# A two-layer graph network on one core: filler by three running sums, another order of groups, and paired products in float32r

## The chip, the core and the metric

The kernel runs on one core of a Trainium2 chip. A core has a matrix engine (PE, whose weight loads are listed apart as PEld), a vector engine (DVE), a scalar engine (ACT), a general engine (POOL), which here starts the indirect gathers, and a sync engine (SP), which starts most other transfers. PE writes to PSUM; the other memory on the chip is SBUF. The metric is the device time of one execution in microseconds (us).

## The reference

12,500 nodes with 256 features, 200,000 edges sorted by their target `dst`. Two layers of the same kind, a last product, the residual and a layer norm:

```python
def _sage_conv(x, src, dst, W_l, b_l, W_r):
    agg = segment_sum(x[src], dst, num_segments=12500)
    deg = segment_sum(ones, dst, num_segments=12500)
    mean = agg / maximum(deg, 1.0)[:, None]
    return mean @ W_l + b_l + x @ W_r

h = relu(_sage_conv(x, src, dst, W1_l, b1, W1_r))
h = relu(_sage_conv(h, src, dst, W2_l, b2, W2_r))
x = layernorm(x + h @ W3 + b3)
```

`dst` is drawn as 12500 u² with u uniform, so low nodes have many edges (the first 256 nodes more than a tenth of all) and high nodes few; `src` is uniform.

## The kernel before

Nodes are handled in 98 blocks of 128. Two ways of summing run side by side.

**Gathers**, for nodes with few edges (from node 1280 in layer 1, from 2048 in layer 2). A round (`Gathers.gathered`) fetches four tiles of 128 source rows with four indirect DMAs from POOL into one of four buffers `got` (L262); then PE multiplies each by a 128 x 32 matrix of ones and zeros into a strip of `part_ps` (L274). ACT copies a finished group to `some` (L284), PE spreads it to nodes (L290), DVE adds it to the ring `sums` (L304). Layer 1 has 269 such rounds (1076 gathers), layer 2 has 235 (940). A buffer is written again once PE's strips of four rounds earlier are done.

**Counts**, for nodes with many edges: groups of 256 target nodes, numbered from 0. `count(g)` builds the matrix C[source node, target node] of how many edges join the two, in bfloat16 as `counts` (98 blocks x 256 columns): per tile of 128 edges DVE makes `pick`, `low` and `aft` by comparison (L738 to L746), PE multiplies them (L765, L776, L780) into `count_ps`, and ACT copies the result into a window of `counts` (L782); for the first 128 tiles DVE adds it instead (L769). The eight groups have 236, 120, 92, 80, 80, 72, 68 and 68 tiles. `product` then sums over the 98 source blocks, rows transposed times C, into `dense_ps` (L707). Rows are float32 values split exactly into three bfloat16 parts by `exact` (two DVE and two ACT steps a block), stored to `x3_d` or `h3_d` in HBM and loaded again two blocks at a time; so each block and group costs six matmuls of 256 columns.

In layer 1, group 0 is counted while all rows of x are split; then group g is counted while the product of group g-1 runs, up to group 5; groups 0 to 4 are multiplied, and the counts of 0 to 3 are stored in HBM (`stored`, L831). Layer 2 makes four passes over the rows of h: pass g (4 to 7) multiplies group g, counted on chip, and beside it group g-4, whose counts are streamed back from HBM (L697), into `beside_ps`; groups 6 and 7 are counted meanwhile.

**Blocks.** When a block's sum is complete, `first_block` or `last_block` runs in pieces: load the rows, transpose on PE (L902), copy on ACT (L904), the products with the weights (L925, L930), bias and degree on DVE (L936, L937), relu on ACT (L939); layer 1 then stores h and its parts, layer 2 goes on with W3 and the layer norm (L993 to L1010).

**The order** on PE and POOL is written out by the program. `layer` goes through the rounds; in each it issues the gathers and strips, and three times takes a piece of a block (`pieces`) and then filler (`fill`): counts, products, splits, taken from generators that yield a cost. The costs are scalars; `mixed` interleaves the parts of a stage in proportion; the whole cost of a layer is spread evenly over its rounds but the last 8 (layer 1) or 14 (layer 2).

Of the kernel before, what the change touches and what calls it, by code (L numbers as in the profile page):

```python
# [1 line left out]

# [5 lines left out]
F32 = mybir.dt.float32  # L8
F16 = mybir.dt.float16
# [38 lines left out]
def by_runs(  # L48
# [66 lines left out]
    def room(t):  # L115
# [16 lines left out]
    h3_d = dram.tile([P, NB, 3, D], BF16, name="h3_d")  # L132
    count_d = dram.tile([HG1 - 1, P, NB, DN], BF16, name="count_d")
# [7 lines left out]
    place = consts.tile([1, len(groups)], I32, name="place")  # L141
# [3 lines left out]
    key_t = [consts.tile([P, n], F32, name=f"key_t{g}") for g, n in enumerate(tiles_of)]  # L145
    after_from = [max(t, FIRST - 1) for t in lows[:HG]]
    after_t = [consts.tile([P, b - a], F32, name=f"after_t{g}")
               for g, (a, b) in enumerate(zip(after_from, highs))]
    offs = [consts.tile([1, n], I32, name=f"offs{g}") for g, n in enumerate(tiles_of)]
# [33 lines left out]
    degs = spare[0:1]  # L183
    rdeg = early.tile([P, NB], F32, name="rdeg")
# [6 lines left out]
    NROWS = 4  # L191
# [114 lines left out]
    with tc.tile_pool(name="setup", bufs=1) as su, \  # L306
# [180 lines left out]
        nxt_first = su.tile([P, HC], F32, name="nxt_first")  # L487
        later(nc.vector.tensor_copy(nxt_first, nxt_i[:, :HC, P - 1]))
        most_c = max(b - a for a, b in spans)
        for g, (c0, c1) in enumerate(spans):  # L490
            n = c1 - c0
            for begins, to, name, since in ((start, key_t[g], "key", lows[g]),
                                            (nxt_first, after_t[g], "aft", after_from[g])):
                at = su.tile([P, HC], F32, name="at", bufs=2)
                nc.vector.tensor_scalar(at[:, :n], begins[:, c0:c1], float(DN * g),
                                        float(DN * (g + 1)), op0=OP.max, op1=OP.min)
                key = su.tile([P, most_c, P], F32, name="key", bufs=2)
                nc.vector.tensor_tensor(key[:, :n], dst_f[:, c0:c1],
                                        at[:, :n].unsqueeze(2).to_broadcast([P, n, P]), op=OP.subtract)
                nc.vector.scalar_tensor_tensor(key[:, :n], key[:, :n], float(NB), high[:, c0:c1],  # L500
                                               op0=OP.mult, op1=OP.add)
                columns(key, (c0, c1), to, name, c0, since, highs[g])

            nc.vector.tensor_scalar(off_f, f1, float(DN * g), float(DN * (g + 1)), op0=OP.max, op1=OP.min)
            nc.vector.tensor_scalar(off_f, off_f, -float(DN * g), None, op0=OP.add)
            nc.vector.tensor_copy(offs[g], off_f[:, lows[g]:highs[g]])
            early_round()
# [64 lines left out]
    w3_sb = weight(w3, "w3_sb", "w3")  # L572

    biases = consts.tile([P, 3, D], F32, name="biases")
    for i, b in enumerate((b1, b2, b3)):
        nc.scalar.dma_start(biases[:, i], b[None, :].to_broadcast([P, D]))
# [9 lines left out]
    split = keep.tile([P, 2, 3, D], BF16, name="split")  # L586
    counts = [keep.tile([P, NB, DN + WIDEST + WIDEST % 2], BF16, name=f"counts{i}") for i in range(2)]
    NEAR = int(at_most(FIRST)) + room(FIRST - 1)
    assert NEAR <= DN
    for c_sb in counts:  # L590
        blank = c_sb.rearrange("p s d -> p (s d)").bitcast(F32)
        nc.scalar.copy(blank, zero.to_broadcast(list(blank.shape)))
# [9 lines left out]
    def layer(gathers, block, n_pieces, dense, dense_cost, left):  # L602
# [3 lines left out]
        turn = 0  # L606

# [7 lines left out]
        def pieces():  # L615
# [5 lines left out]
            if q:  # L621
                next(q[1])
                q[2:] = q[2] - 1, turn + APART
                if q[2] == 0:
                    done.add(q[0])
                    queue.remove(q)
# [3 lines left out]
        spent = 0.0  # L630

        def fill(upto):
            nonlocal spent
            while spent < upto:
                spent += next(filler, 1e9)
# [3 lines left out]
        for i in range(i0, n + 1):  # L639
            before = gathers.step()  # L640

            due = dense_cost * (i + 1 - i0) / (n - i0 - left) if i + 1 < n - left else 1e8
            for part in range(3):
                if part == 2 and before:
                    gathers.summed(*before, done)
                    while begun < left_after(before[0]):
# [3 lines left out]
                fill(spent + (due - spent) / (3 - part))  # L650
        fill(1e8)
# [4 lines left out]
    def exact(t, s, rest):  # L656

# [10 lines left out]
    def split_rows(b):  # L668
        t = load_rows(x, N, b, "split_sb")
        s = split[:, b % 2]  # L670
        leaves = exact(t, s, work.tile([P, D], F32, name="rest", tag="own"))
        if b < 3:
            later(leaves)
        nc.sync.dma_start(x3_d[:, b], s)

    STREAMS = 4
    streams = [spare.bitcast(BF16)[:, i * 2 * DN:(i + 1) * 2 * DN].rearrange("p (b d) -> p b d", b=2)
               for i in range(STREAMS)]
    n_streamed = 0

    def product(table3, g, c_sb, beside=None):


        nonlocal n_streamed
        ps = [dense_pool.tile([P, NC, DN], F32, name="dense_ps")]
        if beside is not None:
            ps.append(beside_pool.tile([P, NC, DN], F32, name="beside_ps"))
        for t in ps:
            nc.tensor.matmul(t, lhsT=zeros_b, rhs=c_sb[:, :NC, :DN], start=True, stop=False)
# [709 lines left out]
```

## Time and profile before

| what | us or share |
|---|---|
| median of 3 runs | 3278.43 (3268.89 to 3285.49) |
| profiled execution | 3281.46, its span 3279.7 |
| granted TensorE clock, mean | 0.888 |
| PE busy | 79% |
| POOL busy | 60% |
| DVE busy | 48% |
| ACT busy | 35% |
| DMA queues q1 (SP) and q0 (POOL) | 34.0% and 26.7% of 16 engines |

Layer 1's rounds begin about 24 us into the span and its last blocks end near 1751; layer 2 begins its gathers at 1753, its products end at 3156. In rows of single instructions the columns are: start and duration in us, engine, line, operation, output <- inputs, and in brackets how long the engine sat idle before it and what ended that. Matmuls overlap, so their durations are longer than their distance from start to start.

### The profile page before, as it was taken

What the parts mean: (1) busy time and instruction counts of PE and PEld (TensorE: products, weight loads), DVE (VectorE), ACT (ScalarE), POOL (GpSimd) and SP (SyncE); (2) the same over time, 40 slices, a digit from 0 to 9 for tenths busy, and PEclk for the clock granted to TensorE, in tenths of its full rate; (3) what the DMA queues carried; (4) which work ended last, traced back from release to release, by engine and by line L of the source; (5) the groups of instructions that cost most, each with busy time, mean ns of one, the idle gap of its engine ahead of it and who ended that gap; (6) DMA issues with size and microseconds to landing.
All of it is one profiled execution on the core that took longest, in us unless ns stands there. A gap on an engine that the chain in (4) does not pass through costs nothing.

```text
span 3279.7 us, 56146 instructions
## 1 busy us (share of the span) xinstructions
PE 2574.5 (79%) x18946; PEld 1733.1 (53%) x18946; DVE 1566.5 (48%) x5560; ACT 1151.6 (35%) x2331; POOL 1967.7 (60%) x2026
## 2 busy tenths in 40 slices
PE   4565668878878878889865887878889888888876
PEld 2122335545546656656643555556556666666654
DVE  6778675544445555555552122334345444343334
ACT  0423664444444444455441001223233333221122
POOL 6665666666665656666664666565666666556652
PEclk9766679979979989989987899989989999999998
DMA  5565668658658758647644566565556656566642
GB/s 123 164 185 171 179 205 274 209 159 262 209 156 289 225 174 266 221 144 238 222 142 122 181 183 184 176 181 166 177 167 192 184 170 183 164 200 198 204 139 84
DMA packets 375242, 612.56 MB, mean 187 GB/s; under 512 B 72111, under 2 KB 253989, under 8 KB 374949
## 3 DMA queue, kind: packets, MB, share of 16 engines
q1 hardware_dynamic: 273235, 343.33, 34.0%
q0 software_dynamic: 96768, 264.37, 26.7%
q8 instruction: 155, 2.54, 0.3%
q10 hardware_dynamic: 4946, 1.19, 0.2%
q14 instruction: 138, 1.13, 0.1%
HBM read 518.75 MB, written 89.92 MB: 186 GB/s over the span
## 4 chain that ended last, share of the span: by engine, by line
PE 59%; issue 8%; another core or an unknown queue 7%; DVE 5%; ACT 3%; DMA 3%; POOL 0%; ACTq 0%; DVEq 0%; SPq 0%; POOLq 0%
PE dense_ps L707 16%; PE part_ps L274 7%; PE count_ps L776 7%; PE beside_ps L707 6%; PE block_ps L925 6%; PE block_ps L930 5%; PE sum_ps L290 4%; PE block_ps L997 3%; PE block_ps L902 3%; DMA rows<-x_d 2%; ACT counts L782 2%; PE count_ps L780 1%; PE sum_ps L296 1%; PE dense_ps L797 1%
## 5 line engine op out<-in xcount | busy, mean ns | idle before, releaser
L262 POOL DMA_INDIRECT got<-in_x_dram,src_t x1076 | 1067.8, 992 | 649.6 <-issue 258.2
L262 POOL DMA_INDIRECT got<-h_d,src_t x940 | 897.7, 955 | 617.1 <-issue 230.8
L707 PE MATMUL dense_ps<-counts,rows 128*128 128x256 bf16 x5292 | 981.6, 282 | 58.9 <-issue 31.5
L707 PEld LDWEIGHTS <-rows 128*128 128x128 bf16 x7644 | 745.2, 101 | 327.6 <-issue 165.6
L782 ACT CAST counts<-count_ps 128x882 f32 (+3 forms) x688 | 611.3, 888 | 533.1 <-PE count_ps L776 135.6
L707 PE MATMUL beside_ps<-spare,rows 128*128 128x256 bf16 x2352 | 570.3, 282 | 24.2 <-issue 23.2
L776 PE MATMUL count_ps<-pick,low 128*128 128x490 bf16 (+2 forms) x1188 | 378.7, 371 | 145.0 <-ACT counts L782 64.3
L274 PE MATMUL part_ps<-got,one 128*32 128x257 f32 (+1 forms) x4032 | 385.4, 434 | 53.2 <-issue 21.7
L738 DVE TENSOR_SCALAR pick<-steps,key_t 128x686 bf16<-128x686 f16 (+3 forms) x816 | 332.6, 410 | 117.6 <-remote 32.1
L218 DVE TENSOR_TENSOR one<-lo_t,lane_b 128x128 f32<-128x128 bf16 x504 | 144.1, 286 | 470.7 <-remote 150.1
L284 ACT COPY some<-part_ps 128x257 f32<-128x257 f32 (+1 forms) x355 | 132.8, 374 | 643.4 <-remote 293.7
L741 DVE TENSOR_SCALAR low<-lanes,low_t 128x130 bf16<-128x130 f16 x816 | 221.0, 272 | 212.4 <-remote 72.5
L304 DVE TENSOR_TENSOR sums<-sums,sum_ps 128x256 f32 x355 | 145.6, 410 | 250.2 <-remote 110.6
L290 PE MATMUL sum_ps<-two,some 128*128 128x128 f32 x1420 | 241.1, 296 | 13.1 <-issue 8.3
L290 PEld LDWEIGHTS sum_ps<-two,some 128*128 128x128 f32 x1420 | 211.2, 207 | 32.2 <-issue 19.3
L776 PEld LDWEIGHTS <-low 128*128 128x128 bf16 x1188 | 121.1, 103 | 181.9 <-issue 62.7
L936 DVE TENSOR_TENSOR own<-block_ps,biases 128x256 f32<-128x256 f32 x196 | 82.4, 420 | 220.3 <-PE block_ps L930 106.5
L274 PEld LDWEIGHTS part_ps<-got,one 128*32 128x32 f32 x4032 | 89.1, 113 | 184.1 <-issue 161.1
L925 PE MATMUL block_ps<-w1l_sb,sums 128*128 128x256 f32 x352 | 123.5, 483 | 69.7 <-issue 31.5
L933 ACT COPY sums<-zero 128x256 f32<-128x256 f32 x170 | 68.7, 404 | 306.0 <-PE block_ps L930 142.6
L904 ACT COPY own_t<-block_ps 128x256 f32<-128x256 f32 x294 | 109.3, 375 | 183.4 <-remote 65.4
L746 DVE TENSOR_SCALAR aft<-steps,after_t 128x98 bf16<-128x98 f16 x689 | 173.6, 252 | 0.0
(184 smaller groups left out, 2678.7 us busy)
## 6 DMA issues: line engine op xcount, KB each, us to landing
rows<-x_d SPq DMA_DIRECT2D x245, 384.0 KB
rows<-h_d SPq DMA_DIRECT2D x196, 384.0 KB
count_d<-counts SPq DMA_DIRECT2D x28, 896.0 KB
spare<-count_d SPq DMA_DIRECT2D x196, 128.0 KB
x_sb<-in_x_dram SPq DMA_DIRECT2D x194, 128.0 KB
x_d<-split SPq DMA_DIRECT2D x98, 192.0 KB
h_d<-split SPq DMA_DIRECT2D x98, 192.0 KB
got<-in_x_dram,src_t POOLq DMA_INDIRECT x1076
```

Of the source, the lines that this page charges most:

```text
L262: rows = nc.gpsimd.indirect_dma_start(out=g[:, j, :D], out_offset=None, in_=self.table, in_offset=bass.IndirectOffsetOnAxis(ap=src_t[:, e: ...
L274: strip = nc.tensor.matmul(part_ps[j * W:(j + 1) * W, :width], lhsT=one[:, j], rhs=g[:, j, :width], start=r == 0, stop=r == n - 1)
L290: nc.tensor.matmul(sum_ps[:, c], lhsT=some[:, c * P:(c + 1) * P], rhs=two, start=True, stop=True)
L304: nc.vector.tensor_add(own, own, sum_ps[:, :NC])
L707: nc.tensor.matmul(t[:, c], lhsT=rows[:, b % 2, k, c * P:(c + 1) * P], rhs=d, start=False, stop=b == NB - 1 and k == 2 and c == NC - 1)
L738: nc.vector.tensor_scalar(r[:, :w * NB], steps[:, :w * NB], key_t[g][:, t - lo_g:t - lo_g + 1], None, op0=OP.is_equal)
L741: nc.vector.tensor_scalar(low.rearrange("p (a b) -> p a b", a=5), lanes_5[:, :, :LW // 5], low_t[:, t:t + 1], None, op0=OP.is_equal)
L746: nc.vector.tensor_scalar(aft.rearrange("p (a b) -> p a b", a=7), steps_7[:, :, :NB // 7], after_t[g][:, t - after_from[g]:t - after_from[ ...
L776: nc.tensor.matmul(c[:, a * NB:b * NB], lhsT=s, rhs=r[:, a * NB:b * NB], start=True, stop=alone)
L782: nc.scalar.copy(to[:, :, bass.ds(off_act.at(t), w)], c.rearrange("p (d s) -> p s d", s=NB))
L925: product = nc.tensor.matmul(ps[:, 0], lhsT=agg[:, c], rhs=wl[:, c], start=c == 0, stop=c == NC - 1)
L930: product = nc.tensor.matmul(ps[:, 1], lhsT=own_t[:, c], rhs=wr[:, c], start=c == 0, stop=c == NC - 1)
```

## The change

1. `layer` keeps three running sums, of PE, DVE and ACT. Rounds, groups, degrees and blocks add to them too; in each third of a round filler is taken until the largest sum reaches a third more of `room_for`, 4.75 in layer 1 and 4.6 in layer 2, which is then taken off all three. Every filler step yields three costs.
2. Layer 1 counts the groups in the order 4, 3, 2, 1, 0, 5. A third of the splits runs beside the count of group 4, the rest beside that of group 3. The product of group 4 (`first_product`) takes no split rows: it multiplies the rows of x in float32 with counts that ACT has copied to float32 (`wide`). The other products are as before. The counts of 4, 3, 2, 1 are stored.
3. In layer 2, `exact` leaves h as two float32 parts, the upper one with its 12 low bits cleared, in `h2_d`. The eight groups are multiplied in pairs, in the order (0, 5), (4, 3), (2, 1), (6, 7): ACT copies the counts of a block for both groups to 512 columns of float32r (`wide`, four buffers), and PE multiplies them with both parts, four matmuls of 512 columns for a block and a pair. Groups 6 and 7 are counted beside the second and third pass.
4. Memory is arranged anew: one tile `tables` for the keys, offsets and places in spare rows, two biases and not three, w3 and b2 loaded at the start of layer 2, `low` and `aft` in four and three buffers for six. The keys of the groups are made from one product for all of them. The counts are no longer cleared as a whole; group 0's columns are, in pieces.

```diff
-    h3_d = dram.tile([P, NB, 3, D], BF16, name="h3_d")
-    count_d = dram.tile([HG1 - 1, P, NB, DN], BF16, name="count_d")
+    h2_d = dram.tile([P, NB, 2, D], F32, name="h2_d")
+    ORDER = [*reversed(range(HG1)), *range(HG1, HG)]
+    SAVED = ORDER[:HG1 - 1] + ORDER[HG1 + 1:HG - 2]
+    count_d = dram.tile([P, NB, len(SAVED), DN], BF16, name="count_d")
...
+    ROUND, GROUP, DEGREE = (0.73, 0.24, 0.0), (0.46, 0.64, 0.37), (0.15, 0.23, 0.0)
...
         def fill(upto):
-            nonlocal spent
-            while spent < upto:
-                spent += next(filler, 1e9)
+            nonlocal over
+            while not over and max(load) < upto:
+                cost = next(filler, None)
+                if cost is None:
+                    over = True
+                else:
+                    spend(cost)
...
             before = gathers.step()
-            due = dense_cost * (i + 1 - i0) / (n - i0 - left) if i + 1 < n - left else 1e8
+            spend(ROUND)
+            whole = room_for if i + 1 < n - left else 1e9
             for part in range(3):
                 if part == 2 and before:
                     gathers.summed(*before, done)
+                    spend(GROUP)
...
                 pieces()
-                fill(spent + (due - spent) / (3 - part))
+                fill(whole * (part + 1) / 3)
+            for e in range(3):
+                load[e] = max(0.0, load[e] - room_for)
...
+    def exact(t, s):
+        leaves = nc.vector.tensor_scalar(s[:, 0].bitcast(I32), t.bitcast(I32), -4096, None,
+                                         op0=OP.bitwise_and)
+        nc.vector.tensor_tensor(s[:, 1], t, s[:, 0], op=OP.subtract)
+        return leaves
...
+    def loaded(b, pair, back):
+        nonlocal n_streamed
+        rows = rows_pool.tile([P, 2, D], F32, name="rows", bufs=N2)
+        freed(nc.sync.dma_start(rows, h2_d[:, b]), back)
+        counted = both[:, b, :, :DN]
+        if pair is not None:
+            counted = streams[n_streamed % STREAMS]
+            n_streamed += 1
+            nc.sync.dma_start(counted, count_d[:, b, pair:pair + 2])
+        return rows, counted
+
+    def widened(counted):
+        wide = rows_pool.tile([P, 2, DN], F32, name="wide", bufs=WIDE)
+        nc.scalar.copy(wide.bitcast(F32R), counted)
+        return wide
...
+    def products(gs, pair):
...
+        for b in range(0, NB, 2):
+            for u in range(b, min(b + 6, NB)):
+                if u not in held:
+                    held[u] = loaded(u, pair, b - (u - N2))
+            for u in range(b, min(b + 4, NB)):
+                if u not in wide:
+                    wide[u] = widened(held[u][1])
+            for u in (b, b + 1):
+                (own, _), of = held[u], wide[u]
+                for k in range(2):
+                    for c in range(NC):
+                        nc.tensor.matmul(ps[c], lhsT=own[:, k, c * P:(c + 1) * P].bitcast(F32R),
+                                         rhs=of.bitcast(F32R), start=u + k == 0,
+                                         stop=u == NB - 1 and k == 1)
+                used.append(len(strips))
+            yield COST_2
...
-    COST_DENSE, COST_DEGREES, COST_SPLIT = 0.7, 1.6, 0.8
+    COST_FIRST, COST_1, COST_2 = (0.92, 0.0, 0.31), (0.68, 0.0, 0.0), (2.06, 0.0, 1.24)
+    COST_DEGREES, COST_SPLIT, COST_REST = (0.4, 0.0, 0.0), (0.0, 0.71, 0.81), (0.0, 0.0, 0.3)
...
-        layer(gathers_1, first_block, 3, staged(stages_1), cost_of(stages_1), 8)
+        layer(gathers_1, first_block, 3, staged(stages_1), 4.75, 8)
...
-    layer(Gathers(h_d, True), last_block, 5, staged(stages_2), cost_of(stages_2), 14)
+    layer(Gathers(h_d, True), last_block, 5, staged(stages_2), 4.6, 14)
```

360 lines of the change are left out of this document (214 added, 146 removed).

## The prediction

> **What bounds the kernel now.** I read the page's first part, then the table by stage, then single engines in order of time. The first part names TensorE:
>
> ```profile
> PE 2574.5 (79%) x18946; PEld 1733.1 (53%) x18946; DVE 1566.5 (48%) x5560; ACT 1151.6 (35%) x2331; POOL 1967.7 (60%) x2026
> ```
>
> The table by stage (us; busy time and instructions of PE, PEld, DVE, ACT, POOL; clock; DMA share; GB/s) says something else. A gather round is four POOL instructions, so POOL's count over four gives the rounds of a stretch.
>
> ```profile
> 110.00:220.00 110.00, 70.24 (x295) 26.77 (x291) 82.88 (x284) 35.89 (x87) 64.05 (x64) 0.66 0.64 191
> 220.00:350.00 130.00, 77.03 (x390) 32.43 (x388) 101.62 (x332) 54.17 (x137) 81.49 (x80) 0.64 0.61 179
> 350.00:478.00 128.00, 83.10 (x400) 37.08 (x399) 90.81 (x367) 81.71 (x178) 76.65 (x79) 0.65 0.61 180
> 478.00:722.00 244.00, 196.48 (x1592) 126.42 (x1590) 126.51 (x531) 114.81 (x207) 153.82 (x158) 0.89 0.68 213
> 722.00:1700.00 978.00, 820.94 (x6638) 567.71 (x6639) 512.57 (x1927) 460.50 (x861) 601.32 (x618) 0.91 0.68 215
> 1760.00:2080.00 320.00, 250.48 (x1857) 169.68 (x1850) 58.14 (x175) 29.20 (x77) 201.10 (x213) 0.88 0.59 179
> 2080.00:2845.00 765.00, 643.48 (x4795) 463.24 (x4794) 319.02 (x1063) 243.89 (x459) 463.44 (x483) 0.92 0.58 175
> 2845.00:3160.00 315.00, 280.81 (x2215) 214.76 (x2214) 119.57 (x364) 64.04 (x181) 188.96 (x200) 0.98 0.64 193
> ```
>
> Per round: 6.60 us in 110 to 478 (55.75 rounds in 368 us; its three lines 6.88, 6.50, 6.48), 6.18, 6.33, then in layer 2 6.01, 6.34, 6.30. In the same lines PE's busy time per round goes from 3.9 to 5.6 us, VectorE's from 1.1 to 5.2, ScalarE's from 0.5 to 4.1. The round hardly moves. So no engine's load sets it; I looked at POOL in order of time:
>
> ```profile
> 1183.70 0.95 POOL L262 DMA_INDIRECT got<-in_x_dram,src_t  x1 [1.07 <-PE block_ps L902]
> 1184.95 0.95 POOL L262 DMA_INDIRECT got<-in_x_dram,src_t  x1 [0.31 <-issue]
> 1186.21 0.95 POOL L262 DMA_INDIRECT got<-in_x_dram,src_t  x1 [0.30 <-issue]
> 1187.46 0.95 POOL L262 DMA_INDIRECT got<-in_x_dram,src_t  x1 [0.30 <-issue]
> 1189.72 0.95 POOL L262 DMA_INDIRECT got<-in_x_dram,src_t  x1 [1.31 <-remote]
> ```
>
> Four gathers start 1.25 us apart, then comes a pause: 6.0 us from round to round, where four times 1.25 would be 5.0. What ends the pause shows best at the start of layer 2 (all engines, in order of time):
>
> ```profile
> 1765.21 0.64 PE L274 MATMUL part_ps<-got,one 128*32 128x256 f32 x8
> ...
> 1776.79 0.95 POOL L262 DMA_INDIRECT got<-h_d,src_t  x1 [0.30 <-issue]
> ...
> 1780.94 0.37 ACT L284 COPY some<-part_ps 128x256 f32<-128x256 f32 x1 [29.47 <-remote]
> 1780.94 0.29 DVE L218 TENSOR_TENSOR one<-lo_t,lane_b 128x128 f32<-128x128 bf16 x1 [19.84 <-remote]
> 1781.17 0.95 POOL L262 DMA_INDIRECT got<-h_d,src_t  x1 [3.43 <-remote]
> ```
>
> PE's second group of strips has ended at 1765.85, yet ScalarE, VectorE and POOL, which all wait for it, go on at 1780.94, after POOL's run of 20 gathers has stopped. In this trace what PE has finished is mostly seen when the gathers pause; and POOL must pause, since the buffer of round i+4 is freed by PE's strips of round i. A run of one round costs 6.1 us, of two 5.95, of five 5.6. That is my reading of the floor: some 500 rounds of 6 us.
>
> **The change part by part.** The profiled execution took 3281.46 us (span 3279.7), 3.0 above the median of the runs, 3278.43. The numbers of gathers (1076 and 940) and of their buffers stay.
>
> *Setup.* The two blankings of counts (22.0 us on ScalarE) go; seven pieces for group 0 come later, beside other work. On VectorE 16 multiply-adds of 0.37 us (5.5) become one of about 1, and the two steps on 768 columns (4.4 and 4.3 us, eight each) run on 68 to 236: some 6 less. Most lies ahead of the first count, where VectorE is 75% busy (82.88 of 110). Taken: -8; ends 0 and -22.
>
> *Order in layer 1.* Group 0 (236 tiles) is no longer counted alone with all 98 splits; group 4 (80 tiles) and a third of the splits begin, and the product of group 4 follows by float32 from x itself. That product has 196 matmuls of two instructions 0.216 us apart (a row of four such, 1.03 us, less the last one's 0.38, over three), 85 us, for 588 bfloat16 ones 0.109 apart (shown below), 64 us: +21 of PE, and 49 copies of 0.59, 29 us of ScalarE. `exact` loses two copies of 0.405 for 98 blocks, -79 us of ScalarE; its VectorE steps stay two. So the rounds loaded by VectorE and ScalarE are fewer and milder. For the first 56 rounds I take 6.33, between 6.48 (350 to 478) and 6.18 (478 to 722): -15 against 6.60; ends -23 and 0.
>
> *Three running sums.* Each round gets work until its fullest engine holds 4.75 us (4.6 in layer 2), the blocks and gathers booked too; before, one scalar was spread evenly. Added up from the costs in the code, no round of layer 1 is then over 4.8 on an engine and the filler is out about 5 rounds ahead of the last 8, so nothing is heaped at the end. The stretches before, with unequal loads, differ little, so evenness buys little: 194 rounds from 6.30 to 6.27, -6. Ends: 6.01 (the quiet stretch), -56; 6.60 (VectorE and ScalarE loaded), +58.
>
> *Pairs and float32r in layer 2.* Per pair and two blocks, 24 matmuls of 256 columns become 8 of 512: 4704 become 1568. Bfloat16 starts 0.109 apart:
>
> ```profile
> 2309.24 0.27 PE L707 MATMUL dense_ps<-counts,rows 128*128 128x256 bf16 x1
> 2309.35 0.27 PE L707 MATMUL beside_ps<-spare,rows 128*128 128x256 bf16 x1
> ...
> 2310.55 0.37 PE L776 MATMUL count_ps<-pick,low 128*128 128x490 bf16 x1
> 2310.76 0.21 PE L780 MATMUL count_ps<-aft,low 128*128 128x98 bf16 x1
> ```
>
> so 4704 cost 513 us. No row shows float32r. Below it is bounded by bfloat16 of 490 columns, 0.21; above by float32, four times as long, 0.86. I take 0.26, near the low end, because the diff splits rows into two 12-bit parts, which a four-pass product wouldn't need, and its own booking is 2.06 for eight: 404 us, 109 less, 0.49 of each of 224 rounds. PE per round falls from 5.24 (1174.8/224) to 4.75, as in 1760 to 2080 (4.70, round 6.01). Against that ScalarE widens 392 times 128x512, by the 0.59 of d_sb (the same shape) 231 us or 1.03 a round, from 1.5 to 2.5; and 722 to 1700 has 2.98 there with rounds of 6.33. Taken 6.10 against 6.25: -34. Ends 6.01, -54, and the rivals below. Rows are 256 KB for a block where 384 KB held two: +25 MB over layer 2, at 180 GB/s some 10% more, hidden while PE waits for landings almost nowhere (13.5 us once). SP issues 588 loads for 392, with the x, h and out transfers queued behind each; buffers reach six blocks ahead, not eight.
>
> *Between and after the layers.* w3, b2 and the second weights are loaded by SP at the seam, where POOL waits 32.7 us for h: 0 to +5, taken 0. The last 14 rounds hold no filler, as before: 0.
>
> Sum: -8 -15 -6 -34 = -63; 3281.5 - 63 - 3 = 3215.
>
> **Rivals.**
> *A, slower: PE waits for the widened counts.* `wide` holds two steps; ScalarE can fill a step only once it has seen PE's step two back. If it sees PE's work once a pause, two steps pass per pause. The first pass, group pair (0, 5), puts 49 steps into 32 rounds, 1.5 a round. With a pause each 6.1 us that suffices; with one every second round (12 us), as in half of 1760 to 2080, 49 steps take 294 us instead of 195: +99, 3314. It decides from 8 us between pauses in that pass. For: the 15 us above. Against: later passes need 0.8 a round, and a waiting PE shortens the runs.
> *B, slower: the weight load shows.* PEld takes 101 ns for bfloat16 (L707) but 207 for float32 (L290). Unhidden, a float32r step is 0.216 + 0.207 = 0.42 each, 663 us, 150 over before, +0.67 a round: about 3278 - 29 + 150 = 3400. Against: float32 products now start 0.216 apart with such loads between. The Trainium skill, page "TensorE: Matmul & The Clock Gate", section "Weight-path perf modes — Fast Weight Load (FWL) and DoubleRow", says that the fast load is for types other than FP32. By that rule B's slow load holds; the rows agree for float32, none shows float32r.
> *C, no change:* the round stays at its floor and only setup and part of the first rounds gain, -8 to -16: about 3268.
> *D, more:* lighter PE lets POOL run two rounds between pauses, 5.97 everywhere: 56 x 0.63 + 194 x 0.33 + 224 x 0.28 = 162, 3108 with the setup; with longer runs (5.6) below 3000.
>
> **How the numbers follow.** Forecast (3150 to 3262) 0.43; D 0.17; C 0.15; A 0.12; B 0.08; 0.05 for rounds of 6.6 in layer 1 (+58). A measurement of this kernel tells about 0.5%, 16 us, from nothing. Faster is the forecast and D, 0.60; same is C, 0.15; slower is A, B and the rest, 0.25. The time is the forecast's, 3215; its own range 3150 to 3262. The range for 8 in 10 goes down into D, to 3060 (0.10 below), and up past A, short of B, to 3360 (0.10 above).
>
> **What would show it.** Right: gathers still 1.25 us apart in fours with a pause of about 1 us; 6.2 to 6.4 us a round in layer 1 and about 6.1 in layer 2, whatever the load; 512-column products about 0.22 to 0.26 us apart; the first dense product before 300 us. A would show as idle PE ahead of the float32r products, released by ScalarE's copies, in the first pass; B as starts 0.4 apart; D as pauses after every second round or fewer. The forecast is wrong if rounds follow the engines' loads after all.

## The result: slightly slower, 1.0074 times the time before

The changed kernel took 3300.02 us (median of 10 runs, 3288.41 to 3307.22), the kernel before 3276.02 beside it on the same chip (10 runs, 3262.2 to 3286.98): ratio 1.0074, 95% interval 1.0057 to 1.0090. The forecast was 3215. The profiled execution took 3297.59, its span 3295.7, 16.0 us more than the profiled one of before. The profile after, first part and then the table by stage (columns as before):

```profile
PE 2444.6 (74%) x15606; PEld 1619.0 (49%) x15606; DVE 1546.7 (47%) x5546; ACT 1334.7 (40%) x2589; POOL 1954.2 (59%) x2026
...
722.00:1700.00 978.00, 773.77 (x5916) 502.30 (x5913) 556.77 (x2122) 378.19 (x698) 578.36 (x600) 0.87 0.62 188
1760.00:2080.00 320.00, 234.17 (x1208) 158.10 (x1209) 79.13 (x256) 115.58 (x231) 196.56 (x207) 0.87 0.66 213
2080.00:2845.00 765.00, 565.80 (x3125) 387.43 (x3123) 303.63 (x1007) 336.94 (x625) 451.03 (x473) 0.90 0.64 199
```

PE has 130 us less to do and ACT 183 more. Yet POOL gets fewer gathers into 722 to 1700 (600 for 618, a round 6.52 us for 6.33), 1760 to 2080 (207 for 213, 6.18 for 6.01) and 2080 to 2845 (473 for 483, 6.47 for 6.34).

The stretches move, so it is better to follow the rounds. From the start of a round's first gather to that of a later one (the first row: from the span's start), both profiled executions, in us:

| part | before | after | difference | my terms |
|---|---|---|---|---|
| up to round 60 of layer 1 | 404.1 | 383.5 | -20.6 | -8, -15 |
| rounds 60 to 180 | 755.0 | 797.0 | +42.0 | |
| rounds 180 to 268 | 556.5 | 559.0 | +2.5 | -6 with the line above |
| seam, to the first gather of layer 2 | 37.4 | 32.5 | -4.9 | 0 |
| layer 2, rounds 0 to 234 | 1477.4 | 1479.0 | +1.6 | -34 |
| from there to the end | 49.3 | 44.6 | -4.7 | 0 |

The floor of a round did fall a little. Rounds of 7.3 us or less last on average 6.07, 6.13, 6.17 (layer 1, rounds 0, 60, 180 on) before and 5.92, 6.05, 6.13 after; in layer 2 (0, 60, 120 to 220) 5.91, 6.06, 6.09 and 5.93, 5.95, 5.98. What took it back is the rounds above 7.3 us: 45 before, 68 after, and their time beyond 6.1 us each is 128 and 186 us. In rounds 60 to 180 of layer 1 there are 20 for 10, 70 us for 20; in 60 to 120 of layer 2, 13 for 5, 35 us for 11.

How such a round comes about, the changed kernel's instructions in order of time (start and duration in us, engine, line, and in brackets the idle time before and its end):

```profile
869.04 0.21 PE L892 MATMUL count_ps<-aft,low 128*128 128x98 bf16 x1
...
872.19 0.79 ACT L894 CAST counts<-count_ps 128x490 f32 x1 [1.11 <-remote]
...
873.04 0.37 PE L888 MATMUL count_ps<-pick,low 128*128 128x490 bf16 x1 [3.13 <-ACT counts L894]
...
874.59 0.25 PE L892 MATMUL count_ps<-aft,low 128*128 128x98 bf16 x1
...
878.20 2.33 ACT L894 CAST counts<-count_ps 128x490 f32 x3 [3.87 <-remote]
...
879.05 0.57 PE L888 MATMUL count_ps<-pick,low 128*128 128x490 bf16 x1 [2.93 <-ACT counts L894]
...
880.91 1.08 PE L286 MATMUL part_ps<-got,one 128*32 128x257 f32 x8
...
882.29 0.94 POOL L274 DMA_INDIRECT got<-in_x_dram,src_t  x1 [6.00 <-PE part_ps L286]
```

PE ends a count product at 869.25; ACT goes on with its result at 872.19. PE ends another at 874.84; ACT goes on at 878.20. `count_ps` has two buffers, so each time the next count product waits for ACT's copy, and the strips stand behind it on PE. They run at 880.91 instead of some 6 us earlier, and POOL, which needs their buffer, stands 6.00 us. The floor is the late sight of PE's work that I had read in the trace; this long round is a hand-over from PE to ACT and back to PE that meets this lateness twice. Not all are of this kind. In each of the 29 rounds over 7.3 us between 60 and 268 of layer 1 POOL waits for the strips, but in the 5 us before that wait and in the wait itself PE stands 0.6 us or more for ACT's count copies in only four of them, for DVE's masks (`pick`, `low`, `aft`) in six, in others for DVE's sums and degrees or at a product's start. Of the 31 in layer 2, PE stands so ahead of a block's transposes in 21, before the change in 10 of 24. PE's waits, before and then after (engine, tile and line, what ended the wait: us, times, longest):

```profile
PE count_ps L776 <- ACT counts L782: 64.3, 52, 9.9
...
PE block_ps L902 <- ACT h L939: 34.6, 29, 3.7
```

```profile
PE count_ps L888 <- ACT counts L894: 116.4, 74, 12.4
PE block_ps L1026 <- ACT own L1062: 81.9, 36, 6.4
...
PE dense_ps L822 <- ACT wide L746: 5.7, 4, 3.1
```

PE's waits for count copies and for the ReLU (`h`, after the change `own`), which it needs for the second transposes of a block, have about doubled. All of PE's waits ahead of these second transposes, also those whose end the profile does not explain, are 51.4 us before and 161.0 after. For the widened counts, my rival A, it hardly waits.

### The profile page after: what moved, and what is told of

The parts are those of the page before. It is cut to its first block, busy times and chain, and to the rows that moved or that the text cites. A ratio compares the mean times of both kernels' runs of the same rounds, so it can differ in the third digit from the quotient of the medians.

```text
span 3295.7 us, 50792 instructions
## 1 busy us (share of the span) xinstructions
PE 2444.6 (74%) x15606; PEld 1619.0 (49%) x15606; DVE 1546.7 (47%) x5546; ACT 1334.7 (40%) x2589; POOL 1954.2 (59%) x2026
## 4 chain that ended last, share of the span: by engine, by line
PE 56%; issue 13%; DVE 8%; another core or an unknown queue 8%; ACT 5%; DMA 5%; POOL 3%; DVEq 1%; SPq 0%; ACTq 0%; POOLq 0%
PE part_ps L286 8%; PE count_ps L888 7%; PE dense_ps L795 7%; PE block_ps L1049 6%; PE dense_ps L822 5%; PE beside_ps L822 5%; PE block_ps L1054 5%; PE sum_ps L302 4%; POOL got L274 3%; PE block_ps L1120 2%; ACT counts L894 2%; PE block_ps L1026 2%; PE dense_ps L775 2%; PE count_ps L877 1%
## 5 line engine op out<-in xcount | busy, mean ns | idle before, releaser
L274 POOL DMA_INDIRECT got<-in_x_dram,src_t x1076 | 1054.8, 980 | 686.8 <-issue 261.0
L888 PE MATMUL count_ps<-pick,low 128*128 128x490 bf16 (+2 forms) x1188 | 386.5, 379 | 274.8 <-ACT counts L894 116.4
L286 PE MATMUL part_ps<-got,one 128*32 128x257 f32 (+1 forms) x4032 | 365.0, 432 | 44.6 <-ACT some L296 21.2
L850 DVE TENSOR_SCALAR pick<-steps,tables 128x686 bf16<-128x686 f16 (+3 forms) x816 | 335.9, 413 | 83.4 <-remote 31.1
L822 PE MATMUL dense_ps<-wide,rows 128*128 128x512 f32 x784 | 365.8, 467 | 11.2 <-ACT wide L746 5.7
L795 PE MATMUL dense_ps<-counts,rows 128*128 128x256 bf16 x2352 | 349.4, 288 | 15.3 <-issue 8.7
L822 PE MATMUL beside_ps<-wide,rows 128*128 128x512 f32 x784 | 333.9, 426 | 0.0
L858 DVE TENSOR_SCALAR aft<-steps,tables 128x98 bf16<-128x98 f16 x689 | 176.5, 256 | 238.1 <-remote 57.8
L795 PEld LDWEIGHTS <-rows 128*128 128x128 bf16 x2352 | 228.6, 103 | 93.8 <-issue 37.9
L888 PEld LDWEIGHTS <-low 128*128 128x128 bf16 x1188 | 120.8, 104 | 214.0 <-issue 93.3
L822 PEld LDWEIGHTS dense_ps<-wide,rows 128*128 128x128 f32 x784 | 167.3, 213 | 70.4 <-issue 22.7
L892 PEld LDWEIGHTS <-low 128*128 128x128 bf16 x681 | 69.3, 102 | 262.8 <-issue 250.3
```

Of the source, the lines that this page charges most:

```text
L274: rows = nc.gpsimd.indirect_dma_start(out=g[:, j, :D], out_offset=None, in_=self.table, in_offset=bass.IndirectOffsetOnAxis(ap=src_t[:, e: ...
L286: strip = nc.tensor.matmul(part_ps[j * W:(j + 1) * W, :width], lhsT=one[:, j], rhs=g[:, j, :width], start=r == 0, stop=r == n - 1)
L795: nc.tensor.matmul(ps[:, c], lhsT=rows[:, b % 2, k, c * P:(c + 1) * P], rhs=c_sb[:, b, :DN], start=False, stop=b == NB - 1 and k == 2 and ...
L822: nc.tensor.matmul(ps[c], lhsT=own[:, k, c * P:(c + 1) * P].bitcast(F32R), rhs=of.bitcast(F32R), start=u + k == 0, stop=u == NB - 1 and k ...
L850: nc.vector.tensor_scalar(r[:, :w * NB], steps[:, :w * NB], key_t[g][:, t - lo_g:t - lo_g + 1], None, op0=OP.is_equal)
L858: nc.vector.tensor_scalar(aft.rearrange("p (a b) -> p a b", a=7), steps_7[:, :, :NB // 7], after_t[g][:, t - after_from[g]:t - after_from[ ...
```

## The experiments

Theories: **P**, three running sums pack work where PE books little; **R**, four and three buffers for `low` and `aft` are too few; **W**, ACT's widening holds up what stands behind it; **S**, a lighter PE meets its transposes too early. The "even filler" below is the changed kernel with the planner of before. All ratios are to the kernel before, on the same chip in the same set of runs.

### Four single edits

```diff
# e1: layer 2 widens the first four pairs of counts only
     def widened(counted):
...
+        if len(fixed) < WIDE:
+            wide = rows_pool.tile([P, 2, DN], F32, name=f"wide{len(fixed)}")
+            nc.scalar.copy(wide.bitcast(F32R), counted)
+            fixed.append(wide)
+        else:
+            fixed.append(fixed[len(fixed) - WIDE])
+        return fixed[-1]
# e2
-            low = work.tile([P, LW], BF16, name="low", bufs=4)
+            low = work.tile([P, LW], BF16, name="low", bufs=6)
-                aft = work.tile([P, NB], BF16, name="aft", bufs=3)
+                aft = work.tile([P, NB], BF16, name="aft", bufs=6)
# e3: spend() books nothing; fill() takes steps while spent < upto and adds max(cost);
# room_for is the whole cost of a layer, 1058.4 and 541.5
-            whole = room_for if i + 1 < n - left else 1e9
+            due = room_for * (i + 1 - i0) / (n - i0 - left) if i + 1 < n - left else 1e9
...
-                fill(whole * (part + 1) / 3)
+                fill(spent + (due - spent) / (3 - part))
# e4: last_block, behind the products
         yield 1.75, 0.77, 0.81
+        yield 0.0, 0.0, 0.0
...
-    layer(Gathers(h_d, True), last_block, 5, staged(stages_2), 4.6, 14)
+    layer(Gathers(h_d, True), last_block, 6, staged(stages_2), 4.6, 14)
```

> The changed kernel, but in layer 2 only the first four pairs of counts are widened; every later float32r product reads those four buffers again. All matmuls, loads and the rest stay, so TensorE does the same and ScalarE loses 388 copies of 0.59 us (229 us of some 560 in layer 2). Left out: the values of layer 2's dense products. Theory W (the loss of layer 2 is ScalarE: its copies into the float32 buffers wait for TensorE and hold up the ReLU and the other copies behind them): layer 2's rounds over 7.3 us go back to the number of before (24 or fewer, excess over 6.1 us about 66 instead of 81 us), the rounds between 60 and 120 fall from 6.57 to 6.25, the whole by 25 to 40 us, to about 0.998 of before. Theory S (TensorE, lighter, reaches the transposes of a block sooner than VectorE and ScalarE can have the rows ready, whoever fills ScalarE): at most 10 us less, 1.004 to 1.008 of before. Theory R and P (the loss is layer 1's alone): 1.005 to 1.008.

> The changed kernel with the buffers of low and aft back at six each, as before the change (four and three in it). Theory R (VectorE can't prepare the masks far enough ahead and TensorE stands in front of the count products, 274.8 us of idle time there against 145.0): layer 1's rounds 60 to 180 fall from 6.64 to about 6.35, so some 35 us, to 0.997 of before; the idle time ahead of count products falls by 100 us or more. Theory P (what is counted when, and how much in one round): no more than 8 us, 1.005 to 1.0075.

> The changed kernel with the planner of before: the filler's largest cost alone is summed and spread evenly over the rounds (1058.4 in layer 1, 541.5 in layer 2), the blocks' and gathers' costs are not booked. The order of the groups, the pairs and float32r stay. Theory P (three sums heap counts, 5.4 to 6.2 tiles a round in rounds 120 to 180, and starve others): layer 1's rounds 60 to 180 fall to 6.4 or less, 25 us or more from the whole, 0.999 of before or less. Theory S and R (what is late is late however the filler is spread): within 10 us of the changed kernel, 1.004 to 1.010. My own forecast's term, that evenness by three sums buys 6 us, would give 1.009.

> The changed kernel; in layer 2 a block has one empty step more between its products with ReLU and the transposes of its result, so that a third of a round more of other work stands before the transposes on TensorE. Theory S (TensorE comes to the transposes too early: 144 us of idle time ahead of them in 1800 to 3180 us, 45 before the change): that idle time falls below 60 us, layer 2's rounds over 7.3 us from 31 to 20 or fewer, layer 2 shorter by 25 to 40 us, 0.996 to 1.000 of before. Theory W: the late ReLU is late still, because ScalarE stands before it; less than 12 us gained, 1.004 or more.

Measured, e1 to e4: 0.9868 (0.9842 to 0.9895), 0.9776 (0.9750 to 0.9802), 0.9774 (0.9749 to 0.9799), 0.9818 (0.9791 to 0.9845). But the kernel before took 2742.68 us here, not 3276: this was another chip, and none of the four expectations was made for it. Nothing could be concluded without the changed kernel there.

### The two kernels on such a chip

> The kernel before, for its profile beside the others. Theory H (TensorE's finished work is told to the other engines late while POOL issues gathers, but not on every chip: in the last runs, on another chip, updates of TensorE's semaphore came 0.01 us after its matmul at the median and 0.04 at nine tenths, where the two profiles of the prediction have 0.4 and 2.6): where its rounds are 6.0 to 6.3 us, half the updates are late by 0.3 us or more and the time is about 3276; where they are 5.0 to 5.2, updates are prompt and the time is about 2743. A rival, theory M (the other chip was faster in its gathers or its clock): the gathers themselves start less than 1.25 us apart there.

> The changed kernel itself. Theory H: where updates are prompt the filler's order and the waits it causes hardly count, rounds are POOL's own 5.0 us, and the change gains what it takes from the first rounds and from rounds held by TensorE: 0.975 to 0.985 of before. Where updates are late: 1.0057 to 1.009 again. If it is not the chip but the edits of the last runs that gained, it is 1.0057 to 1.009 on either.

> The changed kernel without its dense products, except for the first and last block of each (left out: 96 of 98 blocks' products in every pass; loads, widening, counts and the rest stay). TensorE loses about 0.8 to 1.9 of 4.3 to 5.8 us a round. My reading of the floor (it is 4 x 1.25 us and a pause of about 1 us, whatever TensorE has to do, where updates are late): rounds other than the long ones stay at 5.9 to 6.1 us, the whole falls by less than 4%, to about 0.965 to 1.00 of before. The rival (the round follows TensorE's load): rounds of 5.0 to 5.3, 0.83 to 0.87. Where updates are prompt both say 5.0 to 5.1 a round, 0.96 to 0.98 of before.

> The changed kernel with six buffers again for low and for aft, and the filler spread evenly by the planner of before. Where updates are late: theory R and P (the long rounds of layer 1 come from masks and counts that are heaped or not ready): 0.990 to 0.998 of before; theory S and W: 1.000 to 1.008. Where updates are prompt: a little below the changed kernel, by 5 to 15 us, as the two single edits suggest (2682 and 2681 where before took 2743).

The kernel before: 2739.05 us (span 2737.1). The changed kernel 0.9832 (0.9810 to 0.9853), so 43 us faster. Without dense products 0.9788 (0.9758 to 0.9818), rings and even filler together 0.9798 (0.9776 to 0.9820). Theory M falls: gathers start 1.25 us apart here too, and the trace has the same instructions. The granted clock is higher here (0.935 for 0.888), but it doesn't set the round: f3 took 2686.67 us at 0.821. Theory H holds for what ran here; the changed kernel was not run once more with four gathers where updates are late. The changed kernel at the start of layer 2, the place that the prediction showed for before:

```profile
1485.67 0.64 PE L286 MATMUL part_ps<-got,one 128*32 128x256 f32 x8
1485.84 0.94 POOL L274 DMA_INDIRECT got<-h_d,src_t  x1 [0.30 <-issue]
1486.38 0.37 ACT L296 COPY some<-part_ps 128x256 f32<-128x256 f32 x1
1486.38 0.29 DVE L230 TENSOR_TENSOR one<-lo_t,lane_b 128x128 f32<-128x128 bf16 x1 [1.74 <-PE part_ps L286]
1487.09 0.95 POOL L274 DMA_INDIRECT got<-h_d,src_t  x1 [0.30 <-issue]
```

The strips end at 1486.31, ACT and DVE go on at 1486.38, in the middle of a run of gathers; in the first comparison they went on 15 us late. Over a whole trace, from the end of a matmul that raises PE's semaphore to the next update of that semaphore: median 0.01 us and nine tenths within 0.04 here; 0.43 and 2.69 in the first profile of before, 0.36 and 2.58 in that of after (ends of matmuls are modelled; an update up to 0.25 us ahead of one is counted too, and without these it is 0.62 and 2.92, 0.55 and 2.73). I call the chips prompt and late. On a prompt one rounds are 5.0 to 5.2 us, POOL's own four times 1.25, and f3 shows that little else counts: PE's busy time fell from 2236 to 1780 us and the time by 13. Of the 39 us between the two profiled executions of f1 and f2, 28.9 lie ahead of round 60 of layer 1; layer 2's 234 rounds take 1194.1 us for 1195.5, so my largest term brought nothing here either.

### The order of groups, and all edits together

```diff
# g1
-    ORDER = [*reversed(range(HG1)), *range(HG1, HG)]
+    ORDER = [*range(HG)]
# g2: rings of e2, filler of e3, and
-        nc.scalar.activation(own, own, AF.Relu)
+        nc.vector.tensor_scalar(own, own, 0.0, None, op0=OP.max)
```

> The changed kernel with the groups of layer 1 counted from the first up (0, 1, 2, 3, 4, 5) as before the change; so group 0, 236 tiles, comes first again with a third of the splits, its product is the float32 one, and layer 2 pairs (4, 5), then (0, 1), (2, 3), (6, 7). The order is then undone alone. My step 'order in layer 1' says that the first 56 rounds cost 0.27 us more each: 15 us. The traces since say more: without late updates the first 40 rounds took 25 us less with the changed order, with late ones 8 to 20 us less in the first 60, and some of it came back in rounds 60 to 180, where group 0 is now counted. Theory O (the order moves group 0's cost and takes only part of it away): 0 to 15 us slower than the changed kernel, so 0.983 to 0.989 of before where updates are prompt, 1.006 to 1.012 where they are late, with rounds 0 to 60 longer by 20 us or more and rounds 100 to 180 shorter by 10 us or more. Rival (the order is the whole gain): 25 us or more slower, 0.993 or more where updates are prompt.

> The changed kernel with six buffers each for low and aft, the filler spread evenly by the planner of before, and the ReLU of a block on VectorE, behind the additions that feed it, in place of ScalarE. Where updates are late: theory P, R and S (the 24 us come from count products without masks or buffers and transposes that wait for ScalarE's ReLU, and each of the three edits takes one wait away) 0.980 to 0.995 of before; if the long rounds have another cause 1.000 to 1.008. Where updates are prompt: 0.974 to 0.980, as the first two edits gave there (0.9774, 0.9776, together 0.9798), the ReLU nothing.

Prompt again (before 2742.72). g1: 0.9952 (0.9928 to 0.9975), and by its time the rival, "the order is the whole gain". The trace says otherwise. Up to round 60 it is shorter, 332.3 us against 344.5 with the changed order (f2), and at round 260 of layer 1 it is still 11.8 us ahead. Then comes one line of POOL:

```profile
1443.79 0.95 POOL L274 DMA_INDIRECT got<-in_x_dram,src_t  x1 [36.19 <-PE part_ps L286]
```

With the groups in this order the three sums, at 4.75 us a round, have filler left when the last eight rounds begin, and `fill` then takes all of it at once: 36.2 us in which POOL stands, with PE busy 43.0 of the 44 us from 1400 on. So both my theory (the first rounds 20 us longer) and the rival fall; the loss is a heap at the end. The gain of the first 60 rounds, 25 to 41 us in all prompt runs with either order, is therefore not the order's. I take it for the cheaper setup and for two thirds of the splits moved out of that stage, but didn't undo these two alone. g2: 0.9803 (0.9778 to 0.9829), no better than e3.

### The changed kernel and the even filler on one chip

> The changed kernel once more, as the control of the next run on the same chip. Where TensorE's updates are prompt (chip 4: 0.9832, 0.981 to 0.9853): 0.981 to 0.986 of before. Where they are late: 1.0057 to 1.009.

> The changed kernel with the filler spread evenly by the planner of before, beside the changed kernel on one chip. On chip 1 it had 0.9774 of before, and on chip 4 the changed kernel 0.9832; with six buffers and the even filler together it was 0.9798 and 0.9803. Theory P (the three sums cost time, because they pack counts close in the rounds in which TensorE books little): 8 us or more below the changed kernel where updates are prompt; 20 us or more below where they are late, with rounds 60 to 180 of layer 1 at 6.45 or less. Rival (the difference was that of two chips): within 5 us of it.

0.9806 (0.9783 to 0.9828) and 0.9774 (0.9751 to 0.9796), 2694.39 and 2681.8 us: 12.6 us, theory P on a prompt chip. By parts the even filler takes 14 us less up to round 60 of layer 1 and 23 less in 60 to 180, 9 less in 60 to 120 of layer 2, and gives back 11 in rounds 180 to 268, 12 in 120 to 220 of layer 2 and 10 at the seam and the end: it spreads what the sums had packed. PE's waits in front of count products fall from 123.9 to 82.6 us, in front of block products and transposes from 140.3 to 79.8.

So e1 to e4 can be read against 0.9806 and 0.9832. W finds nothing (0.9868, if anything slower, with 226 us less of ACT's time), S no more: e4 took PE's waits for ACT's ReLU from 92.0 us to 0.8 and time 0.9818; other waits took their place (36.1 us for DVE ahead of the W3 products). P and R each gain some 0.4%, R by a reading between chips whose intervals overlap, and f4 and g2, with both, no more than P. All four speak of prompt chips alone, where the changed kernel has 11 rounds over 7.3 us (f2) and not 68; e1 and e4, the tests of W and S, were not run on a late one.

### Three gathers a round

```diff
# i1 on the kernel before, i2 on the changed one, i3 on that of e3
-            for j in range(G):
+            for j in range(1 if i >= NGOT else 0, G):
```

> The kernel before, with three of a round's four gathers from the fifth round of each layer on (left out: the first strip's gather, whose rows stay those of an earlier round). POOL then needs 3.75 us a round, so that something else must set the round. Theory T (TensorE then does, as my sums of its work say): about 5.2 us a round in layer 2 with updates that are prompt, TensorE 95% busy or more, the time hardly below before, 0.96 to 1.00. Rival (the engines could follow): below 0.92. Where updates are late: 3.75 and a pause of 1.1, about 4.9 a round, if TensorE's load let it.

> The same of the changed kernel. My steps said that TensorE has 0.49 us less to do in a round of layer 2, and waits nothing for the widened counts. If that holds where POOL isn't the bound: layer 2 (235 rounds) 80 to 115 us shorter than in the run before it. If TensorE waits for ScalarE and VectorE instead (57 waits of 1.4 us before the transposes in 1560 to 2600 us with four gathers): less than 50 us shorter.

> The same of the changed kernel with the filler spread evenly. If the three sums cost time by what they heap, not by POOL: 10 to 30 us below the run before it again; if POOL's pauses made that difference: within 8 us.

These fell on a late chip (before 3282.58 us). 0.8496 (0.8480 to 0.8513), 0.8515 (0.8488 to 0.8543), 0.8347 (0.8324 to 0.8370): 2789.87, 2790.85 and 2742.68 us. The kernel before, POOL in layer 2:

```profile
2202.64 0.94 POOL L262 DMA_INDIRECT got<-h_d,src_t  x1 [1.44 <-PE part_ps L274]
2203.89 0.95 POOL L262 DMA_INDIRECT got<-h_d,src_t  x1 [0.31 <-issue]
2205.15 0.95 POOL L262 DMA_INDIRECT got<-h_d,src_t  x1 [0.30 <-issue]
2207.26 0.95 POOL L262 DMA_INDIRECT got<-h_d,src_t  x1 [1.17 <-PE count_ps L776]
```

Three gathers and a pause: the median round is 4.84 us in layer 1 and 4.81 in layer 2, where four had 6.1. With PE's work unchanged, 15% of the time goes. That is the reading of the floor that the prediction stood on, n times 1.25 and about 1.1, and it is shown for a late chip. The mean in layer 2 is 5.19: in rounds 60 to 220 PE is 94 to 97% busy and comes close to setting the round, as theory T had it.

My largest term falls here. Layer 2's 234 rounds take 1214.0 us before, 1273.9 after, 1228.5 after with the even filler. So the changed kernel is 60 us longer where I had said 80 to 115 shorter, or less than 50 shorter; but 45 of the 60 go with the three sums, which cost 48 us in the whole, more than the 10 to 30 that I gave. PE's longest waits in layer 2, of i1, i2 and i3:

```profile
PE block_ps L902 <- ACT h L939: 22.9, 12, 3.5
...
PE block_ps L1026 <- ACT own L1062: 87.7, 34, 5.4
...
PE block_ps L1024 <- ACT own L1060: 46.3, 32, 5.1
```

In rounds 60 to 120 PE is 94% busy in i1, at 5.08 us a round, so lighter work could have shown. In i2 it is 78% busy at 5.93 us and waits 33.6 us for the ReLU; in i3, with the same products, 81% busy at 5.12 us and 7.2. The stand of i2 is the sums', and without them the lighter products win nothing.

### Four gathers on a late chip

> The changed kernel with the filler spread evenly, all four gathers. Where updates are late: with three gathers it took 48 us less there than the changed kernel (2742.7 and 2790.9); theory P: 25 to 50 us less with four, 0.990 to 0.999 of before against 1.0074, long rounds (over 7.3 us) of layer 1's rounds 60 to 180 down from 20 to 12 or fewer. Rival (with four gathers the pauses hide it): 1.003 to 1.009. Where updates are prompt: 0.977 again.

> The changed kernel with the even filler, six buffers each for low and aft, and the ReLU of a block on VectorE. Where updates are late the even filler alone had 0.9992 of before (0.997 to 1.0014); its trace still has 131.5 us of TensorE waiting for ScalarE's count copies, 49.1 for VectorE's masks and 51.7 for ScalarE's ReLU. If the masks' buffers and the ReLU have a share: 0.985 to 0.996, with the waits for masks and for the ReLU's row below 25 us each. If what is late is the update, whoever sends the rows: 0.997 to 1.002, the waits turning up elsewhere. Where updates are prompt: 0.980 again.

> The changed kernel without its dense products, except the first and last block of each (left out: 96 of 98 blocks' products in every pass), all four gathers. Where updates are late: my floor (4 x 1.25 us and a pause of 1.0 to 1.1, whatever TensorE has to do; with three gathers the commonest round was 4.8) keeps the median round at 5.9 to 6.1 us, and only the long rounds go, at most some 100 us: 0.965 to 1.00 of before. The rival (the round follows TensorE's load, which falls by a fifth to a third): rounds of 5.0 to 5.4, 0.85 to 0.90. Where updates are prompt: 0.979 again.

j1 (e3's kernel), late chip, before 3281.92: 0.9992 (0.9970 to 1.0014), 3283.53 us. Against 1.0074 in the first comparison the even filler brings 0.8%, some 27 us, at the weak end of what P said; the chip need not be that one. Profiled executions, long rounds being those over 7.3 us:

| part | before | changed | even filler |
|---|---|---|---|
| rounds 60 to 180 of layer 1, us | 755.0 | 797.0 | 765.1 |
| rounds 180 to 268, us | 556.5 | 559.0 | 576.6 |
| layer 2, rounds 0 to 234, us | 1477.4 | 1479.0 | 1468.5 |
| long rounds, 60 to 180 and 180 to 268 | 10 and 5 | 20 and 9 | 15 and 16 |
| long rounds, layer 2 | 24 | 31 | 33 |
| PE waits for count copies, us | 64.3 | 116.4 | 131.5 |
| PE waits ahead of second transposes, us | 51.4 | 161.0 | 83.9 |

So the time falls, but the long rounds have moved and not gone (where I said 12 in 60 to 180, 15 are left), and PE's waits for count copies are no shorter. As far as profiles of two sets of runs tell, the sums are a part of the loss, and something else in the change brings most of the long rounds.

k1 (g2's kernel), late, before 3247.23: 1.0035 (1.0011 to 1.0058), outside what either theory gave. Waits for `low` fell from 58.6 to 14.7 us, but those for the ReLU's row went over with it from ACT to DVE and grew, from 51.7 to 97.8 us (j1, then k1):

```profile
PE block_ps L1024 <- ACT own L1060: 51.7, 24, 6.5
...
PE block_ps L1024 <- DVE own L1060: 97.8, 31, 9.9
```

PE's waits ahead of block products and transposes are 327.2 us in all, 289.5 in j1. R has no share there that can be measured, nor has moving the ReLU; that the waits turn up elsewhere is what I had said for updates that are late whoever sends the rows. This is the chip of the runs with three gathers, where the kernel before had taken 3282.58: from one set of runs to the next it moved by 1.1%, more than the change is worth. So what is read between sets, as j1 against the first comparison, is weaker than the 12.6 and 48 us that were read within one. k2 fell on a prompt chip: 0.9772 (0.9736 to 0.9807), as f3. The floor without dense products on a late chip stays unmeasured.

No version with all its work beats the kernel before on a late chip with four gathers: the even filler is among the best on prompt chips (2681 for 2743) and level with before on a late one.

## Why the prediction was wrong

**The bound** was right: rounds of four gathers and a pause, not an engine's load. But I took it for the kernel's; it is that of the kernel on a late chip.

**Setup and first rounds**, -8 and -15: measured -20.6. The size is right, the reason for the second half not: g1 keeps the gain with the order undone, on a prompt chip. (VectorE's 82.88 of 110 us, which I gave for the time ahead of the first count, is that of 110 to 220; from 0 to 110 it is 79.12.)

**Three running sums**, -6: this step failed. "Evenness buys little: 194 rounds from 6.30 to 6.27" became 6.52 in rounds 60 to 268, +44.5 us. I reasoned that stretches with unequal loads differ little; that looks at means, and rounds over 7.3 us grew from 15 to 29. Against the even filler the sums cost 12.6 us on a prompt chip, 48 with three gathers a round, and some 27 on a late chip with four (read between two sets of runs): a cost where I booked a gain. It lay inside the ends that I gave (-56 to +58), and the rival of rounds of 6.6, which rounds 60 to 180 came to (6.64), had 0.05. But the sums are not the whole: with the even filler rounds 60 to 268 still take 30 us more (j1 against the first profile of before, both with late updates), with 31 long rounds and 131.5 us of waits for count copies. Group 0's 236 tiles, formerly first, are now counted beside dense products in this part. That is my likeliest cause; it is not shown on a late chip.

**Pairs and float32r**, -34: failed, +1.6. The sizes were right. Products in float32r, in order of time:

```profile
2192.84 0.40 PE L822 MATMUL beside_ps<-wide,rows 128*128 128x512 f32 x1
2193.08 0.39 PE L822 MATMUL dense_ps<-wide,rows 128*128 128x512 f32 x1
2193.30 0.40 PE L822 MATMUL beside_ps<-wide,rows 128*128 128x512 f32 x1
```

0.23 us apart where I took 0.26. What failed is "PE per round falls from 5.24 to 4.75, as in 1760 to 2080 (4.70, round 6.01)": I took a quiet stretch for one with light PE. It is quiet because next to nothing is counted there and few blocks run. PE's load did fall, to 4.71 us a round (1035.8 us over 220 rounds, 1760 to 3160), and the round didn't follow: 6.32 for 6.31. Rounds up to 7.3 us fell by 0.1 us in 60 to 220, some 17 us, and the long rounds gave it back. The even filler tells how much of this is the sums': with it layer 2 took 1468.5 us (j1), 9 less than before and not 34, and with three gathers 1228.5 for 1214.0 (i3 and i1). So the lighter products bought next to nothing under either planner; that is shown. Why is argued: the work that I called PE's load was also the cover of the way from a block's products over DVE and ACT to its transposes, and with it gone PE waits there. Most of that wait went with the sums, though (161.0 us, 83.9 with the even filler, 51.4 before), and neither e4 nor k1 won time by an edit at the ReLU.

**Seam and tail**, 0: -4.9 and -4.7.

**Rivals.** A is refuted in its place (5.7 us of waits) and half right in its kind: PE's waits for ACT did grow, at the count copies and the ReLU, but that they took the gain is not shown. B is refuted: 0.23 apart, not 0.4. The weight load of these products takes 213 ns, twice bfloat16's 103 and near float32's 208 (means of the changed kernel's profile); with starts 0.23 us apart it was hidden under 512 columns. The Trainium skill (page "TensorE: Matmul & The Clock Gate", section "Weight-path perf modes — Fast Weight Load (FWL) and DoubleRow") says that the fast load isn't for FP32; the load's own row agrees, if float32r counts as FP32 there. C came nearest in mechanism: the floor stays but for 0.1 us, the gain of the first rounds remains; it had no term for the long rounds. D didn't come.

## What to carry to other kernels

Where a round has a floor, count the rounds that break it, with what they wait for: means of a stretch hide that twice as many do. Before booking lighter work on an engine as time, ask whether that engine sets the round, and look for the hand-overs to other engines and back that the work now covers. Compare a planner that fills each round to its brim with an even spread of the same filler before believing it: here the packing cost 12.6 us on one kind of chip and 48 in a run with fewer gathers. And when an edit takes a wait away, look where it turns up again. Measure on more than one chip before a small term is believed: here the sign of the change hung on it.

## What the runs showed of the hardware

The kernel before took 2743 to 2747 us (medians) on five chips and 3247 to 3283 on two, besides 3276 in the first comparison, with equal gathers (1.25 us from start to start) and like bytes. What differs is when an update of PE's semaphore comes after its matmul: 0.01 us at the median and 0.04 at nine tenths on the one kind, about 0.4 and 2.6 on the other with four gathers a round (0.5 to 0.6 and 2.7 to 2.9 without the allowance of 0.25), where the updates crowd between 5.75 and 6.75 us after a round's first gather, about POOL's pause. With three gathers a round a tenth are later than 1.6 to 1.75 us, and the median is 0.03 (0.1 to 0.2 and 1.8 to 1.9 without it). On the prompt chips POOL issues gathers almost without a pause (16.6 us of waits for strips in 1560 to 2600 of f2) and no update is held. So POOL's gathers alone don't do it; what in those chips does stays open. The change is 0.981 to 0.983 of before on the one kind and 1.0074 on the other.
